# A third table of sums, another order of the last experts, and stores issued from ScalarE

## The chip, the core and the metric

The kernel runs on one core of a Trainium2 chip. The core has TensorE (PE: matrix products and transposes), VectorE (DVE), ScalarE (ACT), GpSimd (POOL) and SyncE (SP), and sixteen DMA engines between its SBUF and HBM. SP, ACT and POOL can issue transfers, each from its own queue and in the order of that queue. An instruction that waits holds up all that stands behind it on its engine. The metric is the time of one execution on the device, in microseconds (us); lower is better.

## The reference, cut to what matters

The input `x` has 4 x 512 tokens of 512 numbers, float32. Four layers are added to it one after the other: an expert with quantised weights, an FFN whose weights come from a table of 16 numbers, a state-space scan, and last a mixture of 32 experts, which is what the change touches:

```python
probs = softmax(x @ gate_w);  w, sel = top_k(probs, 8);  w = w / sum(w)
# each token is sent to its 8 experts; xg holds the tokens of expert e
g = einsum("ech,ehi->eci", xg, w_gate)
u = einsum("ech,ehi->eci", xg, w_up)
y = einsum("eci,eih->ech", silu(g) * u, w_down)
out = zeros.at[t_slot].add(w_slot[:, None] * y)   # summed by token
return x + out
```

An expert's inner width is 192. Each token is in eight experts, so every row of the result is `x` plus eight weighted rows `y`.

## The kernel before, in words

The tokens lie in SBUF as `x[128, 16, 512]`: sixteen tiles of 128 tokens. Batches 0 and 1 are the lower half (tiles 0 to 7), batches 2 and 3 the upper half (tiles 8 to 15). Early in the kernel, between the table lookups of the FFN's weights (`lut_weights`), `scratch` makes the tables in HBM that the experts' results are summed in, and `clear` writes zeros into them (L677 to L686): six stores of three tiles for each table, kept in SP's program order.

An expert's work is a generator, `expert` (L877), in four stages: (1) SP loads its weights and POOL gathers its tokens' rows from `xln` in blocks of 128 (`xg`); (2) TensorE transposes each block, ACT and VectorE in turn copy it to `exT`; (3) TensorE forms gate and up products in PSUM, ACT applies a tanh (L941), and VectorE does two multiplications (L942, L943) to get `h`; (4) TensorE multiplies `h` with the down weights (L954, L958), ACT (even blocks, L967) or VectorE (odd blocks, L965) scales the rows by the gates into `ey`, and POOL scatters them, adding, into a table of sums in HBM (L968). The scatters of one expert come in the order of blocks 0, 2, 1, 3, 4 in the code (a group is multiplied together), for three blocks 0, 1, 2. Two scatters into one table wait for one another, the second being issued when the first has landed; two tables, used by even and odd blocks, take turns.

Experts 0 to 7 are run twice. The first part, with the tokens of the lower half (at most 320 places), runs early beside the routing of the last batch. The second part takes the tokens of the upper half, again 320 places: three blocks. The other 24 experts run once with 576 places, five blocks. The list `calls` (L1125 to L1127) holds the 24 full experts and the eight second parts: 8, 0b, 9, 1b, ..., 15, 7b, and then 16 to 31. `pipeline` (L977) steps through them: for each call the loads of the call two further on and stage 3, then the transposes of the next call and stage 4.

At the end, each token's sum has to be added to `x` and the result stored. The last five and a part of the last but one expert's scatters are put into `sums[1]` (L1129), so that `sums[0]` is complete sooner. `weave` (L1134) then mixes the last expert's two steps with `add_sums(tp, 0, False)`: eight pieces of two tiles, each read from `sums[0]` by SP into a buffer `acc` (six buffers) and added to `x` by VectorE (L1003). `add_sums(tp, 1, True)` follows when the last scatter has landed: eight pieces of `sums[1]`, read by SP (L999), added to `x` into the buffer `acc`, and stored from there by SP (L1005).

The order of the code is not yet that of an engine. A planner takes the instructions, estimates from costs of its own when each will be ready, and writes one fixed list for each engine: among instructions that it thinks ready, the one earlier in the code goes first. On the chip each engine goes through its list in order, waiting where data is not there. A DMA is an entry in the list of the engine that issues it.

```python
sums = [two] * (len(calls) - 2) + [two[:4] + k.sums[1:], k.sums[1:] * 5]
run(islice(late, 2 * len(calls) - 2))
weave((late, 2), (k.add_sums(tp, 0, False), NT // 2))
run(k.add_sums(tp, 1, True))
```

After all this the kernel reads a flag and, only if some expert had more tokens than places, would do the layer anew (`in_full`).

Of the kernel before, what the change touches and what calls it, by code (L numbers as in the profile page):

```python
# [16 lines left out]
F32 = mybir.dt.float32  # L17
# [5 lines left out]
ALU = mybir.AluOpType  # L23
# [4 lines left out]
P = 128  # L28
NB = 4
S = 512  # L30
HID = 512
NT = NB * S // P
# [16 lines left out]
SLOTS = 576  # L49
EARLY = 8  # L50
ROOM = (320, 320)
LO = 32
ROW = HID + NE
LN_EPS = 1e-5
# [5 lines left out]
class Kernel:  # L60
# [556 lines left out]
    def routing_constants(self, rp):  # L617
# [31 lines left out]
        nc.vector.memset(self.room, float(SLOTS))  # L649
        for g, n in enumerate(ROOM):  # L650
            nc.vector.memset(self.room[:, g, :EARLY], float(n))
# [8 lines left out]
    def scratch(self, c):  # L660

        nc = self.nc

        self.xln = [
            self.dram.tile([n * S + 1, ROW], F32, name=f"xln{g}") for g, n in enumerate((NB // 2, NB))
        ]
        zero = c.tile([P, ROW], F32, name="zero")
        nc.vector.memset(zero, 0.0)
        for xln in self.xln:
            nc.sync.dma_start(out=xln[0:1, :], in_=zero[0:1, :ROW])  # L670

        self.sums = [self.dram.tile([NB * S + 2 * P, HID], F32, name=f"sums{i}") for i in range(2)]
        self.kept = self.dram.tile([NB * S, HID], F32, name="kept")
        yield
        yield from self.clear(zero)

    def clear(self, zero):  # L677

        nc = self.nc
        for s in self.sums:  # L680
            for a in range(0, NT + 2, 3):
                z = nc.sync.dma_start(
                    out=s.rearrange("(a p) d -> p a d", p=P)[:, a : a + 3, :],
                    in_=zero[:, :HID].unsqueeze(1).to_broadcast([P, 3, HID]),
                )
                self.tc.keep_in_program_order(z)  # L686
                yield
# [302 lines left out]
            next(e)  # L990
            yield

    def add_sums(self, tp, i, out):

        nc = self.nc
        for a in range(0, NT, 2):
            s = tp.tile([P, 2, HID], F32, tag="acc", name="acc")
            r0 = 1 + a * P
            nc.sync.dma_start(  # L999
                out=s, in_=self.sums[i][r0 : r0 + 2 * P, :].rearrange("(i p) d -> p i d", p=P)  # L1000
            )
            x = self.x[:, a : a + 2, :]
            nc.vector.tensor_tensor(s if out else x, s, x, ALU.add)  # L1003
            if out:
                nc.sync.dma_start(  # L1005
                    out=self.t["out"].rearrange("b (i p) d -> p (b i) d", p=P)[:, a : a + 2, :], in_=s
                )
            yield

    def in_full(self, rp, ep, tp):  # L1010

        nc = self.nc
        zero = ep.tile([P, 2 * HID], F32, tag="exT", name="zero")
        nc.vector.memset(zero, 0.0)
        run(self.clear(zero))
        nc.sync.dma_start(out=self.x, in_=self.kept.rearrange("(i p) d -> p i d", p=P))
        table = ep.tile([P, NE // 4, CAP // LO], F32, tag="xg", name="table", bufs=10)
        nc.vector.memset(table, 0.0)
        for b in range(NB):
            run(self.place(rp, b, self.mask(rp, self.one_hot(rp, b)), self.seen[1], table, None))  # L1020
        toks = self.slots(rp, [table], 0, NE, CAP, "f")
        for e0 in range(0, NE, NE // 2):
            at = self.slot_tokens(rp, toks[:, :, e0 : e0 + NE // 2], CAP, "f")
            run(
                self.pipeline(
                    self.expert(ep, e, (self.xln[1], *at, lo // P), e - e0, HID, self.sums[:1] * 5)
                    for e in range(e0, e0 + NE // 2)
                    for lo in range(0, CAP, HID)
                )
            )  # L1030
        run(self.add_sums(tp, 0, True))


def run(steps):
    for _ in steps:
        pass
# [15 lines left out]
def weave(*streams):  # L1052

    streams = [[0, n, g] for g, n in streams]
    while streams:
        s = min(streams, key=lambda s: s[0] / s[1])
        s[0] += 1
        if next(s[2], StopIteration) is StopIteration:
            streams.remove(s)


@with_exitstack
def tile_kernel(ctx: ExitStack, tc: tile.TileContext, t: dict):
    k = Kernel(tc, t)
    k.constants(ctx)
    scan = ExitStack()
    with ExitStack() as early:
        with ExitStack() as ffn:
            wp = ffn.enter_context(tc.tile_pool(name="wp", bufs=1, side="right"))
            with ExitStack() as first:  # L1070
                k.banks(first, t=2, m=2, y=2, d=2)
                ap = first.enter_context(tc.tile_pool(name="ap", bufs=2))
                sq = staggered([k.smooth_quant(ap, b) for b in range(NB)], 15)
                with ExitStack() as lut:
                    lc = lut.enter_context(tc.tile_pool(name="lc", bufs=1, side="right"))
                    lp = lut.enter_context(tc.tile_pool(name="lp", bufs=2, side="right"))
                    k.lut_tables(lc, wp)
                    lookups = k.lut_weights(lp, k.jobs)
                    weave((islice(sq, 40), 40), (islice(lookups, 48), 48))
                    k.tile_rows(wp, lc)  # L1080
                    weave((islice(sq, 48), 48), (lookups, 4 * len(k.jobs) - 48), (k.scratch(lc), 14))

                pp = ffn.enter_context(tc.tile_pool(name="pp", bufs=1, side="right"))
                k.scan_weights(pp)
                k.prep_tag = "y"
                preps = 2 * KH + 1
                weave((k.prepare(pp, pp, 0), preps), (sq, 30 * NB - 88))
            k.banks(early, t=2, m=2, y=1, d=3)
            k.prep_tag = "t"
            bp = ffn.enter_context(tc.tile_pool(name="bp", bufs=2, side="right"))  # L1090
            rp = ctx.enter_context(tc.tile_pool(name="rp", bufs=1))
            mp = scan.enter_context(tc.tile_pool(name="mp", bufs=2))
            k.routing_constants(rp)
            steps = (TPB // 2) * (NIC + 3)
            units = KH * 16
            routes = 2 * (TPB + 1)

            ffn_ = chain(*(k.lut_ffn(bp, b) for b in range(NB)))
            run(islice(ffn_, 4))
            for b in range(NB):  # L1100
                n = steps
                streams = [(k.scan(mp, b), units), (islice(ffn_, n), n)]
                if b + 1 < NB:
                    streams.append((k.prepare(pp, (pp, mp)[(b + 1) % 2], b + 1), preps))
                if b:
                    run(k.gate(mp, b - 1))
                    streams.append((k.route(rp, b - 1), routes))
                if b == NB - 1:
                    tok = k.slots(rp, k.tables[:1], 0, EARLY, ROOM[0], "a")
                    at = k.slot_tokens(rp, tok, ROOM[0], "a")  # L1110
                weave(*streams)
        ep = ctx.enter_context(tc.tile_pool(name="ep", bufs=2, side="right"))
        k.gu_tag = "m"
        full, nc = SLOTS // P, tc.nc
        two = [k.sums[j % 2] for j in range(full + 1)]
        first = k.pipeline(k.expert(ep, e, (k.xln[0], *at, 0), e, ROOM[0], two) for e in range(EARLY))
        weave((chain(k.gate(mp, NB - 1), k.route(rp, NB - 1)), KH + routes), (first, 2 * EARLY))
    scan.close()
    k.banks(ctx, t=4, g=4)
    k.gu_tag = "g"  # L1120
    tp = ctx.enter_context(tc.tile_pool(name="tp", bufs=6))
    at = k.slot_tokens(rp, k.slots(rp, k.tables, EARLY, NE, SLOTS, "u"), SLOTS, "u")
    at_b = k.slot_tokens(rp, k.slots(rp, k.tables[1:], 0, EARLY, ROOM[1], "b"), ROOM[1], "b")
    k.overflow(rp)
    calls = [(e, at, e - EARLY, SLOTS) for e in range(EARLY, NE)]  # L1125
    for e in range(EARLY):
        calls.insert(2 * e + 1, (e, at_b, e, ROOM[1]))  # L1127

    sums = [two] * (len(calls) - 2) + [two[:4] + k.sums[1:], k.sums[1:] * 5]  # L1129
    late = k.pipeline(  # L1130
        k.expert(ep, e, (k.xln[1], *at, 0), col, n, s) for (e, at, col, n), s in zip(calls, sums)
    )
    run(islice(late, 2 * len(calls) - 2))
    weave((late, 2), (k.add_sums(tp, 0, False), NT // 2))  # L1134
    run(k.add_sums(tp, 1, True))
    more = nc.values_load(k.more[0:1, 0:1], min_val=0, max_val=1)  # L1136
    with tc.If(more):
        k.in_full(rp, ep, tp)
# [51 lines left out]
```

## Time and profile before

| | us |
|---|---|
| median of 3 runs | 1964.97 (1963.19 to 1970.44) |
| profiled execution | 1967.59 |
| its span, first to last instruction | 1965.8 |
| TensorE busy in the span | 1667.2 (85%) |
| VectorE busy | 1192.7 (61%) |
| GpSimd busy | 999.0 (51%) |
| ScalarE busy | 712.7 (36%) |
| last expert's last output written by ACT | 1915.68, for 0.68 |
| last scatter issued | 1929.31 |
| first read of the final eight pieces | 1933.10 |

A time in the profile is counted from the start of the span. A line of a timeline gives start, duration, engine, line of the code, operation, the tile written and the tiles read, how many, and in brackets the idle time before it and what ended that. A line of the chain gives start, duration, and what the end of the kernel waited for in that stretch. In the forty slices of the page each digit is a tenth of busy share; `PEclk` is the clock that TensorE was granted, and a slice is 49 us long. DMA busy time is not that of an instruction: the line of a DMA on an engine's queue is its issue, and the data lands later.

### The profile page before, as it was taken

To read this page: it belongs to the slowest core of one execution; us is meant where nothing else is said; L and a number is where in the kernel's file an instruction comes from. 1 tells how busy PE (TensorE), PEld (TensorE's weight loads), DVE (VectorE), ACT (ScalarE), POOL (GpSimd) and SP (SyncE) were. 2 spreads that over 40 slices of the span, in tenths; PEclk is the share of its full clock that TensorE was granted. 3 is DMA by queue.
4 is the path that set the end of the run, shared out by engine and by line. 5 is a ranking of instruction groups with operands and counts; after the bars stand their busy time and mean duration, and the time that the engine had idled before them with its cause. 6 is when DMAs were issued, how large, how long until landed. Compare 5 with 4: busy or idle time off the path is not lost. (4 is left out here: it accounts for less than half of the span.)

```text
span 1965.8 us, 25002 instructions
## 1 busy us (share of the span) xinstructions
PE 1667.2 (85%) x8845; PEld 984.2 (50%) x8845; DVE 1192.7 (61%) x2029; ACT 712.7 (36%) x1345; POOL 999.0 (51%) x824
## 2 busy tenths in 40 slices
PE   4778775899889888888799688799999999999980
PEld 2444332556454545454555344455556566556540
DVE  6887864788799979999889634422222233222231
ACT  1554455535443554355433322222222222222210
POOL 3110113768755875478566543556555555555420
PEclk9889986899999998899999799999999999999985
DMA  9524510889887888788789686688888877877656
GB/s 264 140 80 153 182 50 34 221 201 227 211 234 165 208 212 213 165 200 205 207 198 221 189 210 134 165 180 197 176 181 178 185 164 160 180 169 170 111 128 186
DMA packets 187673, 346.69 MB, mean 176 GB/s; under 512 B 41698, under 2 KB 88130, under 8 KB 187540
## 3 DMA queue, kind: packets, MB, share of 16 engines
q1 hardware_dynamic: 147332, 251.96, 48.6%
q0 software_dynamic: 39952, 92.66, 23.7%
q8 instruction: 72, 1.18, 0.3%
q10 hardware_dynamic: 256, 0.39, 0.1%
q14 instruction: 61, 0.50, 0.1%
HBM read 277.08 MB, written 76.32 MB: 180 GB/s over the span
## 5 line engine op out<-in xcount | busy, mean ns | idle before, releaser
L968 POOL DMA_INDIRECT sums<-ey,to x168 | 260.8, 1552 | 311.5 <-DMA sums<-ey,to 123.4
L925 PE MATMUL pg<-exT,egu 128*128 128x320 f32 (+1 forms) x1536 | 402.5, 419 | 15.5 <-DVE eh L943 7.6
L563 POOL TENSOR_TENSOR dBu<-d,BC 128x512 f32<-128x512 f32 x256 | 330.8, 1302 | 112.1 <-DMA d<-dts 79.8
L925 PEld LDWEIGHTS pg<-exT,egu 128*128 128x128 f32 x1536 | 289.2, 191 | 131.8 <-issue 38.0
L568 DVE TENSOR_TENSOR_SCAN st<-st,dBu 128x512 f32<-128x512 f32 x192 | 230.7, 1218 | 29.9 <-POOL dBu L563 25.3
L561 ACT ACTIVATE st<-d,A 128x512 f32<-128x512 f32 x256 | 173.5, 689 | 189.9 <-DVE sc L569 122.1
L375 PE MATMUL pgu<-xT,wg 128*128 128x256 f32 (+1 forms) x704 | 189.4, 412 | 30.6 <-DVE h L385 26.1
L900 POOL DMA_INDIRECT xg<-xln,tokens x168 | 162.0, 964 | 90.8 <-issue 37.9
L942 DVE SCALAR_TENSOR_TENSOR eh<-eh,pg 128x320 f32<-128x320 f32 (+5 forms) x144 | 61.1, 425 | 230.6 <-ACT eh L941 229.3
L954 PE MATMUL po_e<-ed,eh 128*128 128x512 f32 (+1 forms) x336 | 172.9, 633 | 13.2 <-ACT ey L967 6.2
L340 PE MATMUL pw<-oh,lut_t 128*32 128x344 bf16 (+1 forms) x2052 | 127.0, 359 | 65.5 <-DVE oh L334 65.2
L375 PEld LDWEIGHTS pgu<-xT,wg 128*128 128x128 f32 (+1 forms) x704 | 132.3, 198 | 97.3 <-DVE h L385 39.0
L375 PE MATMUL pgu<-xT,wu 128*128 128x256 f32 (+1 forms) x704 | 179.4, 397 | 0.0
L967 ACT ACTIVATE ey<-po_e,gates 128x512 f32<-128x512 f32 (+1 forms) x104 | 68.8, 684 | 303.8 <-PE po_e L958 151.1
L965 DVE TENSOR_SCALAR ey<-po_e,gates 128x512 f32<-128x512 f32 x64 | 45.9, 748 | 209.0 <-PE po_e L958 209.0
L391 PE MATMUL po_f<-wd,h 128*128 128x512 f32 (+1 forms) x352 | 159.8, 610 | 2.6 <-DVE h L385 2.2
L375 PEld LDWEIGHTS pgu<-xT,wu 128*128 128x128 f32 (+1 forms) x704 | 138.5, 199 | 25.8 <-issue 2.9
L569 DVE TENSOR_TENSOR sc<-st,BC 128x512 f32<-128x512 f32 x192 | 127.7, 681 | 19.8 <-PE py L579 18.9
L573 POOL TENSOR_TENSOR sc<-sc,BC 128x512 f32<-128x512 f32 x64 | 83.2, 1300 | 110.0 <-DVE sc L566 83.1
L958 PE MATMUL po_e<-ed,eh 64*128 64x512 f32 (+1 forms) x336 | 114.8, 638 | 0.0
L340 PEld LDWEIGHTS <-lut_t 128*32 128x32 bf16 x2052 | 56.3, 102 | 113.2 <-issue 74.0
L391 PEld LDWEIGHTS po_f<-wd,h 128*128 128x128 f32 (+1 forms) x352 | 68.0, 196 | 86.3 <-issue 80.6
(260 smaller groups left out, 2195.0 us busy)
## 6 DMA issues: line engine op xcount, KB each, us to landing
d<-dts SPq DMA_DIRECT2D x256, 512.0 KB, 6.3
egu<-in_w_gate SPq DMA_DIRECT2D x40, 384.0 KB, 3.8
ix<-idx_b SPq DMA_DIRECT2D x16, 688.0 KB, 5.4
egu<-in_w_up SPq DMA_DIRECT2D x40, 256.0 KB, 5.2
ed<-in_w_down SPq DMA_DIRECT2D x40, 256.0 KB, 4.0
ed<-in_w_down SPq DMA_DIRECT2D x80, 128.0 KB, 4.5
sums<-zero SPq DMA_DIRECT2D x12, 768.0 KB, 6.7
dts<-dt POOLq DMA_DIRECT2D x16, 512.0 KB, 4.5
```

The costliest lines, as they stand in the source:

```text
L340: nc.tensor.matmul(pt[i][32 * c : 32 * c + 32, :step], lhsT=self.lut_t[:, j, g, :], rhs=oh[:, c * n + i * step : c * n + (i + 1) * step], ...
L375: nc.tensor.matmul(pg[:m, j * W : (j + 1) * W], lhsT=w[:, k, c * P : c * P + m], rhs=xT[:, k, :], start=k == 0, stop=k == KH - 1,)
L391: nc.tensor.matmul(po, lhsT=h[:m, c, i * P : (i + 1) * P], rhs=self.wd[:m, c, :], start=c == 0, stop=c == NIC - 1,)
L561: nc.scalar.activation(st, d[:, 0, :], AF.Exp, scale=self.A[:, i : i + 1])
L563: product = nc.gpsimd.tensor_tensor(dBu, d[:, 1, :], BC[:, 0, :], ALU.mult)
L568: nc.vector.tensor_tensor_scan(st, st, dBu, 0.0, ALU.mult, ALU.add)
L569: nc.vector.tensor_tensor(sc, st, BC[:, 1, :], ALU.mult)
L900: nc.gpsimd.indirect_dma_start(out=xg[:m, :], out_offset=None, in_=xln, in_offset=bass.IndirectOffsetOnAxis(ap=tokens[:m, lo + j, col : co ...
L925: nc.tensor.matmul(pg[i][:, :hs], lhsT=w[:, k, i * P : (i + 1) * P], rhs=xT[:, k, z : z + hs], start=k == 0, stop=k == KH - 1,)
L954: nc.tensor.matmul(po[j][:m, :], lhsT=h[:, 0, b : b + m], rhs=wd[:, 0, :], start=True, stop=False)
L958: nc.tensor.matmul(po[j][:m, :], lhsT=h[r : r + R, 1, b : b + m], rhs=wd[r : r + R, 1, :], start=False, stop=True)
L968: nc.gpsimd.indirect_dma_start(out=sums[j], out_offset=bass.IndirectOffsetOnAxis(ap=to[:m, lo + j, col : col + 1], axis=0), in_=y[:m, :], ...
```

## The change

A third table `sums[2]` is made, and only its last twelve tiles of rows are cleared (`a0 = NT // 2 - 2` tiles are skipped), which takes four stores; `clear` so has sixteen steps instead of twelve, and the weave that spreads them counts 18 in place of 14. The second parts of experts 6 and 7 (`LAST = 2`) leave their places in the list and come at its very end, after expert 31: the list is 8, 0b, ..., 13, 5b, 14, 15, 16, ..., 31, 6b, 7b. All scatters of these two, three blocks each, go into `sums[2]`; all others, expert 31's too, take turns between `sums[0]` and `sums[1]`. Since second parts hold only tokens of the upper half, the rows of the lower half are then complete in the first two tables.

`add_sums` takes a list of tables and a range of tiles. It now always adds into `x`, table after table, and where it stores, it stores from `x` and issues the store on ACT's queue instead of SP's. The last two calls' four steps are woven with eight pieces: four of the lower half, which add both tables and store, and four of the upper half, which add both tables only. What follows when the last scatter has landed is four pieces of the upper half: read from `sums[2]`, added and stored. `in_full` calls the new form.

```diff
+LAST = 2
-        self.sums = [... for i in range(2)]
+        self.sums = [... for i in range(3)]
...
-        for s in self.sums:
-            for a in range(0, NT + 2, 3):
+        for s, a0 in zip(self.sums, (0, 0, NT // 2 - 2)):
+            for a in range(a0, NT + 2, 3):
...
-    def add_sums(self, tp, i, out):
+    def add_sums(self, tp, sums, a0, a1, out):
-        for a in range(0, NT, 2):
-            s = tp.tile([P, 2, HID], F32, tag="acc", name="acc")
-            r0 = 1 + a * P
-            nc.sync.dma_start(out=s, in_=self.sums[i][r0 : r0 + 2 * P, :]...)
+        for a in range(a0, a1, 2):
             x = self.x[:, a : a + 2, :]
-            nc.vector.tensor_tensor(s if out else x, s, x, ALU.add)
+            for table in sums:
+                s = tp.tile([P, 2, HID], F32, tag="acc", name="acc")
+                r0 = 1 + a * P
+                nc.sync.dma_start(out=s, in_=table[r0 : r0 + 2 * P, :]...)
+                nc.vector.tensor_tensor(x, s, x, ALU.add)
             if out:
-                nc.sync.dma_start(out=self.t["out"]...[:, a : a + 2, :], in_=s)
+                nc.scalar.dma_start(out=self.t["out"]...[:, a : a + 2, :], in_=x)
...
-                    weave(..., (k.scratch(lc), 14))
+                    weave(..., (k.scratch(lc), 18))
...
-    for e in range(EARLY):
+    for e in range(EARLY - LAST):
         calls.insert(2 * e + 1, (e, at_b, e, ROOM[1]))
+    calls += [(e, at_b, e, ROOM[1]) for e in range(EARLY - LAST, EARLY)]
-    sums = [two] * (len(calls) - 2) + [two[:4] + k.sums[1:], k.sums[1:] * 5]
+    sums = [two] * (len(calls) - LAST) + [k.sums[2:] * 3] * LAST
...
-    run(islice(late, 2 * len(calls) - 2))
-    weave((late, 2), (k.add_sums(tp, 0, False), NT // 2))
-    run(k.add_sums(tp, 1, True))
+    run(islice(late, 2 * (len(calls) - LAST)))
+    weave(
+        (late, 2 * LAST),
+        (
+            chain(k.add_sums(tp, k.sums[:2], 0, NT // 2, True), k.add_sums(tp, k.sums[:2], NT // 2, NT, False)),
+            NT // 2,
+        ),
+    )
+    run(k.add_sums(tp, k.sums[2:], NT // 2, NT, True))
```

More of the change, by code (lines that the diff above doesn't have):

```diff
@@ L670, in scratch @@
             nc.sync.dma_start(out=xln[0:1, :], in_=zero[0:1, :ROW])
-        self.sums = [self.dram.tile([NB * S + 2 * P, HID], F32, name=f"sums{i}") for i in range(2)]
+        self.sums = [self.dram.tile([NB * S + 2 * P, HID], F32, name=f"sums{i}") for i in range(3)]
         self.kept = self.dram.tile([NB * S, HID], F32, name="kept")
@@ L991, in pipeline @@
             yield
-    def add_sums(self, tp, i, out):
+    def add_sums(self, tp, sums, a0, a1, out):
         nc = self.nc
-        for a in range(0, NT, 2):
-            s = tp.tile([P, 2, HID], F32, tag="acc", name="acc")
-            r0 = 1 + a * P
-            nc.sync.dma_start(
-                out=s, in_=self.sums[i][r0 : r0 + 2 * P, :].rearrange("(i p) d -> p i d", p=P)
-            )
-            x = self.x[:, a : a + 2, :]
-            nc.vector.tensor_tensor(s if out else x, s, x, ALU.add)
+        for a in range(a0, a1, 2):
+            x = self.x[:, a : a + 2, :]
+            for table in sums:
+                s = tp.tile([P, 2, HID], F32, tag="acc", name="acc")
+                r0 = 1 + a * P
+                nc.sync.dma_start(out=s, in_=table[r0 : r0 + 2 * P, :].rearrange("(i p) d -> p i d", p=P))
+                nc.vector.tensor_tensor(x, s, x, ALU.add)
             if out:
-                nc.sync.dma_start(
-                    out=self.t["out"].rearrange("b (i p) d -> p (b i) d", p=P)[:, a : a + 2, :], in_=s
+                nc.scalar.dma_start(
+                    out=self.t["out"].rearrange("b (i p) d -> p (b i) d", p=P)[:, a : a + 2, :], in_=x
                 )
@@ L1030, in in_full @@
             )
-        run(self.add_sums(tp, 0, True))
+        run(self.add_sums(tp, self.sums[:1], 0, NT, True))
 def run(steps):
@@ L1080, in tile_kernel @@
                     k.tile_rows(wp, lc)
-                    weave((islice(sq, 48), 48), (lookups, 4 * len(k.jobs) - 48), (k.scratch(lc), 14))
+                    weave((islice(sq, 48), 48), (lookups, 4 * len(k.jobs) - 48), (k.scratch(lc), 18))
                 pp = ffn.enter_context(tc.tile_pool(name="pp", bufs=1, side="right"))
```

## The prediction

> **What bounds the kernel now.** I read four views, from the coarse to the fine. First the page's forty slices: TensorE is busy from start to end and then stops in the last slice but one.
>
> ```profile
> PE   4778775899889888888799688799999999999980
> PEclk9889986899999998899999799999999999999985
> DMA  9524510889887888788789686688888877877656
> ```
>
> One slice is 49 us, so the change, which touches the last 90 us, is judged there and not by shares of the span. Second, the chain of work that ended last, in order of time: it holds no arithmetic but one kind of addition.
>
> ```profile
> 1923.70 1.55 DMA sums<-ey,to
> 1929.31 3.73 DMA sums<-ey,to
> ...
> 1934.06 5.57 DMA acc<-sums
> ...
> 1942.79 6.91 DMA acc<-sums
> ...
> 1951.47 5.23 DMA acc<-sums
> ...
> 1958.11 1.23 DVE acc L1003
> ```
>
> The end is set by scatters waiting for one another (to 1933.0), then by eight pieces of a table read, added and stored (to 1959.75), then 6.05 us to the end of the span. Third, POOL's timeline, which shows the scatters of two full experts: number 29 undisturbed, and from 1890.97 those that all go to `sums[1]`.
>
> ```profile
> 1855.48 1.55 POOL L968 DMA_INDIRECT sums<-ey,to  x1 [3.30 <-ACT ey L967]
> 1860.85 1.55 POOL L968 DMA_INDIRECT sums<-ey,to  x1 [3.82 <-issue]
> 1862.71 1.55 POOL L968 DMA_INDIRECT sums<-ey,to  x1 [0.30 <-DVE eh L943]
> 1866.36 1.45 POOL L968 DMA_INDIRECT sums<-ey,to  x1 [2.09 <-DMA sums<-ey,to]
> 1868.65 1.58 POOL L968 DMA_INDIRECT sums<-ey,to  x1 [0.85 <-DVE eh L943]
> ...
> 1890.97 1.55 POOL L968 DMA_INDIRECT sums<-ey,to  x1 [4.41 <-DMA sums<-ey,to]
> 1899.92 1.42 POOL L968 DMA_INDIRECT sums<-ey,to  x1 [7.40 <-DMA sums<-ey,to]
> ```
>
> Two scatters into one table start 5.4 to 5.6 us apart on quiet DMA (1855.48 to 1860.85; 1923.70 to 1929.31), but 8.95 and 6.65 us apart while eight table reads pass (1890.97, 1899.92, 1906.57). I call this a link. Fourth, the timeline of all engines where those reads begin.
>
> ```profile
> 1888.02 9.79 SPq L999 DMA_DIRECT2D acc<-sums  x8
> 1894.61 1.23 DVE L1003 TENSOR_TENSOR x<-acc,x 128x1024 f32<-128x1024 f32 x1 [9.98 <-DMA acc<-sums]
> 1896.34 4.64 PE L925 MATMUL pg<-exT,egu 128*128 128x320 f32 x8 [5.27 <-DVE eh L942]
> ```
>
> The planner put the first addition ahead of products of the last expert. On the chip its data came 6.6 us after the read was issued, VectorE stood still for 9.98 us, TensorE for 5.27, and its granted clock fell from 1.00 (1870 to 1881) to 0.80 (1881 to 1916). This costs little now, since the scatters end later anyway; the same pattern matters more after the change.
>
> **The change, part by part.** *Third table and its clearing:* four more stores of 768 KB, each 0.59 us of SP and landing in a median 6.7 us. They stand between index loads that SP issues 6 to 12 us apart, with DMA at 0.55 from 142 to 246 us. Bounds: nothing, to 4 x 2.3 = 9 us if the DMA engines were the limit there (768 KB at the 330 GB/s of the tail). I take nothing, hidden by the lookups' TensorE and VectorE work.
>
> *Order:* the second parts of experts 6 and 7 leave their places after experts 14 and 15. TensorE's work is the same. Pairs leave it idle 0.2 us in 210, full experts in a row 3.7 in 170 (about 0.5 each, behind the h products); two more in a row cost +1.0 us. When does the last full expert end? Its gate and up products start at 1881.3 now, after eight second parts. One such part is 6.7 (gate, up) + 1.4 (transposes) + 5.0 (down) = 13.1 us, so the start becomes 1881.3 - 26.2 - 0.9 (three transposed blocks stand before it instead of five, for the next call's transposes follow) + 1.0 = 1855.2. Add 11.9 gate and up, 1.4 transposes, 8.1 down: T = 1877.
>
> *When both old tables are complete:* expert 29 ended on TensorE at 1859.4 and its fourth scatter landed about 1871.8 (1866.36 + 5.4), its fifth 1873.9. So `sums[0]` is complete at T + 12.4 = 1889.4 and `sums[1]` at 1891.5. The first read starts about where it does now (1888.0), but TensorE is then deep in the last two second parts rather than in the last full expert.
>
> *Reads and additions beside them:* sixteen reads of 512 KB and four stores, 10.5 MB, where before there were eight reads. At 330 GB/s (what the DMA row shows in slices of this stretch; 512 KB takes 1.6 us) a lower piece takes 4.8 us, an upper piece 3.3. First addition at 1889.4 + 6.6 = 1896, the last at 1896 + 4 x 4.8 + 4 x 3.3 = 1928. A DVE addition itself takes 1.23.
>
> *What is queued behind these waits.* On VectorE the additions stand in the planner's order among the last two experts' products, transposed copies and odd outputs. On ACT four new stores are issued (an ACT issue took 0.31 us, by the row of `xdbl`), each waiting for both additions of its piece; behind them stand the tanh and even outputs that feed the scatters. Before, stores waited on SP alone. Unheld, the first output of expert 6 would be ready at T + 11.8, 1889. Held by the first store, which wants the second or third addition, it comes at 1901 and its scatter at 1902. That is the uncertain value: 1889 to 1902; I take 1902, since the planner showed its optimism about these very reads. Similarly expert 7's products: at one addition per 1.3 us (the alternation with h products in the trace suggests that the planner counts so) some eleven additions precede the last of them, done on the chip at 1896 + 8 x 2.4 + 3 x 1.6 = 1920. The down products then run at half clock (10 us instead of 5), the first output at 1926.5.
>
> *The last chain:* six scatters into `sums[2]`, with the loaded link as the mean of 8.95 and 6.65 = 7.8: 1902, 1909.8, 1917.6; then, when expert 7's output is there, 1926.5, 1933.2, 1938.7; landed 3.75 later, S = 1942.4. Now it is 1933.0.
>
> *The last pieces:* four instead of eight, 4.2 MB instead of 8.4. SP, waiting now in its queue for additions before it may issue more reads, has only reads to issue.
>
> ```profile
> SPq L1005 <- DVE acc L1003: 18.1, 8, 5.0
> ```
>
> The Trainium skill speaks against this step: "DMA: Bandwidth & Descriptors", section "Issuing engines are not separate DMA queues", says that all engines' DMAs run on the same sixteen DMA engines and that a second issuer saves only the time to issue. By that rule I keep the row's pace: 3.8 to the first addition, 4 x (1959.75 - 1936.85) / 8 = 11.5, then 6.05, sum 21.3. By the 18.1 us of waiting I could let all four reads land by +8 (three additions now start 3.8, 5.0 and 6.5 us after the reads): last addition done +9.3, stored +9.6, end +15.7. But the rule's shared engines must still move 4.2 MB, 12.7 us, plus 1.9 to start and the 4.1 between the last traffic and the span's end: 18.7. I take 18; now it is 32.8.
>
> *Sum:* 1942.4 + 18 = 1960.4 against the execution's span of 1965.8: -5.4. Around that span lie 1.8 us (1967.59 in all), which stay. The median of the runs is 2.6 below that execution; I take the difference to the median: 1964.97 - 5.4 = 1959.6, rounded to 1959.
>
> **The rivals.** *Unheld:* the planner leaves expert 6's outputs and expert 7's products ahead of additions and stores. For it: reads wait for scatters that by the planner's own count come after expert 6's products. Against it: the 9.98 us stall. Then the chain starts at 1889 and is bound by links alone: 1889, 1898, 1904.6, 1912.4, 1920.2, 1928, landed 1931.8, end 1949.8: 1949.
>
> *Slower:* the additions stand on VectorE ahead of expert 7's copy of its transposed tokens. All sixteen are done at 1928; then 0.7 for the copy, 13.5 gate and up at half clock, 1.5 products, 7.5 to the first output: scatter at 1951, two more links of 5.5 and 3.75, S = 1966, end 1984, time 1983. It decides against the change from the point where expert 7's first scatter starts later than 1965.8 - 18 - 3.75 - 11 = 1933. If only the products of h are behind all additions, the scatter is at 1937 and the time 1969. For it: VectorE takes instructions in order, and additions were put among products before. Against it: so were products among additions.
>
> *Nothing moves:* the shorter final part (32.8 to 18) is given back by a chain that lands 14.8 us later, at 1948, if every loaded link is 9 us and the first scatter starts after 1905. This lies at the upper end of my own case.
>
> **How the numbers follow.** Faster or slower means 0.5% (9.8 us), about what a measurement of this kernel can tell: below 1955.1 or above 1974.8. My case has 0.50: of it 0.18 faster, 0.31 within, 0.01 slower; its own range is 1951 to 1969, from the loaded link (6.6 to 9 us) and the last part (15.7 to 21.3). Unheld 0.26: 0.25 faster, 0.01 within. Slower mechanism, whole or in part, 0.24: 0.03 within, 0.21 slower. Sums: 0.43, 0.35, 0.22. The range leaves out a little below the unheld case and the worst of the slower one: 1947 to 1976.
>
> **What would show it.** Right: twelve clearing stores become sixteen with no later end of that stage; the last TensorE work well after 1900 at a reduced clock; ACT's longest waits on its own stores; six scatters 6 to 9 us apart, the last landing near 1942; 18 us from there to the end. Wrong: the first of these six at 1889 (unheld), or the fourth later than 1933 (slower); an end of the lookups that moves by several us; or a planner that orders the middle of the kernel anew, which no row here shows.

## The result, and the profile after

The changed kernel takes 1955.16 us, the median of 13 runs (1946.71 to 1964.62), against 1965.36 us (1962.65 to 1976.34) for the kernel before in as many runs. The ratio is 0.9942, with a 95% interval of 0.9924 to 0.9959: 0.6% faster, 10 to 11 us. The profiled execution spans 1953.5 us where the one before spanned 1965.8.

The slices of the page differ at the end: TensorE's last work is now spread out further, and the DMA engines stay busy (0.7 and 0.6 in the last two slices against 0.5 and 0.6 before).

```profile
PE   4778875899889888898888588899999999999981
PEclk9989986899999898899899799999999999999995
DMA  9535611889887887778789696688887877778776
...
sums<-zero SPq DMA_DIRECT2D x16, 768.0 KB, 6.6
```

The sixteen clearing stores cost nothing that can be seen: the last lookup product is at 272.4 us here and was at 275.4 before; over all profiles of this document it lies between 275.4 and 279.7 with twelve stores and between 272.4 and 280.9 with sixteen. The tail is another thing. The chain of what ended last, in order of time (start, duration, what was waited for), from the last full expert on:

```profile
1876.50 5.16 DMA sums<-ey,to
...
1882.39 5.40 DMA sums<-ey,to
...
1887.81 3.62 DMA acc<-sums
...
1891.52 1.24 DVE x L1004
...
1892.78 0.46 ACTq L1006
...
1893.36 0.70 ACT ey L969
...
1894.32 8.65 DMA sums<-ey,to
...
1903.70 7.92 DMA sums<-ey,to
...
1912.36 7.34 DMA sums<-ey,to
...
1920.43 4.71 DMA sums<-ey,to
...
1925.87 4.84 DMA sums<-ey,to
...
1931.44 3.58 DMA sums<-ey,to
...
1936.65 9.21 DMA acc<-sums
```

Read it from the top: the last scatter into `sums[1]` by expert 31 lands at 1887.8; the first piece's read from that table waited for it; its addition lets ACT issue the first store (L1006); only behind that store does ACT write expert 6's first output (L969), and then six scatters follow one another. The last lands at 1935.0, and 18.5 us later the span ends. Before, the last landing was at 1933.0 with 32.8 us to go. So the last part became 14.3 us shorter and the chain landed 2.0 us later; part of the 12.3 us between the two spans arose earlier, as the next section shows.

How the last two experts were held is seen in the timeline of all engines (start, duration, engine and line; in brackets the idle time before and what ended it):

```profile
1889.01 1.22 DVE L1004 TENSOR_TENSOR x<-acc,x 128x1024 f32<-128x1024 f32 x1 [8.80 <-DMA acc<-sums]
1890.15 0.68 DVE L917 COPY exT<-pt_g 128x512 f32<-128x512 f32 x1
1890.89 9.19 PE L927 MATMUL pg<-exT,egu 128*128 128x320 f32 x24 [4.97 <-DVE exT L917]
1892.78 0.46 ACTq L1006 DMA_DIRECT2D out<-x  x1
1893.36 0.69 ACT L969 ACTIVATE ey<-po_e,gates 128x512 f32<-128x512 f32 x1 [12.00 <-DVE x L1004]
```

VectorE stood 8.80 us in front of the first addition, with expert 7's transposed copy behind it; TensorE lost 4.97 us there and did the 24 products in 9.19 us where the same 24 took 6.73 for expert 6. ACT stood for 12.00 us until the second addition released the store. Not all of that is the hold: by the prediction's estimate an output that nothing holds would have come 11.8 us after the last full expert's end, at 1884.8 here, so about 8.5 us are.

### The profile page after: what moved, and what is told of

Read it like the earlier page. It is cut to its first block, busy times and chain, and to the rows that moved or that the text cites. A ratio compares the mean times of both kernels' runs of the same rounds, so it can differ in the third digit from the quotient of the medians.

```text
span 1953.5 us, 25018 instructions
## 1 busy us (share of the span) xinstructions
PE 1661.3 (85%) x8836; PEld 983.6 (50%) x8845; DVE 1196.9 (61%) x2033; ACT 711.6 (36%) x1345; POOL 1001.9 (51%) x824
## 4 chain that ended last, share of the span: by engine, by line
PE 35%; DMA 7%; DVE 5%; issue 2%; ACT 1%; POOL 1%; SPq 0%; ACTq 0%; POOLq 0%; DVEq 0%
PE pg L927 17%; PE po_e L956 8%; PE po_e L960 5%; PE pt_g L915 3%; DMA sums<-ey,to 2%; DMA xg<-xln,tokens 2%; DMA d<-dts 2%; DVE st L569 1%; DVE sc L570 1%; DMA acc<-sums 1%; POOL xg L902 0%; POOL dBu L564 0%; DVE lo_i L803 0%; PE pl L712 0%; DVE eh L945 0%
## 5 line engine op out<-in xcount | busy, mean ns | idle before, releaser
L944 DVE SCALAR_TENSOR_TENSOR eh<-eh,pg 64x128 f32<-64x128 f32 (+5 forms) x144 | 61.1, 425 | 223.5 <-ACT eh L943 222.4
L969 ACT ACTIVATE ey<-po_e,gates 128x512 f32<-128x512 f32 (+1 forms) x104 | 68.7, 684 | 290.2 <-PE po_e L960 143.4
L392 PEld LDWEIGHTS po_f<-wd,h 128*128 128x128 f32 (+1 forms) x352 | 68.3, 197 | 87.3 <-issue 80.3
```

The source lines that it names most:

```text
L392: nc.tensor.matmul(po, lhsT=h[:m, c, i * P : (i + 1) * P], rhs=self.wd[:m, c, :], start=c == 0, stop=c == NIC - 1,)
```

## The experiments

Executions of one kernel differ by more than ten us (the runs above), and the profiles show that much of it arises before the tail, so I also give, for each profile, the time from a **mark** to the end of the span. The mark is the start of the gate and up products of expert 6's second part: 1873.0 in the changed kernel, 1889.3 in another that is the same up to there. For kernels with another order the mark is worked out from the prediction's stage lengths (before: 1881.3 - 26.2 - 0.9 + 11.9 + 1.4 + 8.1 = 1875.6; with one or three second parts at the end, 13.15 us before or after the first one's start). A blank stands where the chain that ended last does not hold the last scatter. Each ratio is to the kernel before as it ran beside that version.

| kernel | ratio to before, interval | mark to end | of it after the last landing |
|---|---|---|---|
| before | 1 | 90.2 | 32.8 |
| order alone | 0.9995, 0.9969 to 1.0022 | 85.7 | 33.0 |
| stores from ACT alone | 0.9985, 0.9965 to 1.0006 | 85.2 | 28.3 |
| changed | 0.9942, 0.9924 to 0.9959 | 80.5 | 18.5 |
| changed, again | 0.9953, 0.9927 to 0.9980 | 79.5 | 15.8 |
| changed, stores from SP | 0.9961, 0.9940 to 0.9981 | 81.5 | 20.8 |
| changed, three read buffers | 0.9940, 0.9916 to 0.9963 | 80.8 | 17.1 |
| additions behind the experts | 0.9913, 0.9880 to 0.9946 | 72.0 | 15.5 |
| the same, ten buffers | 0.9912, 0.9879 to 0.9945 | 72.9 | |
| the same, two tables at the end | 0.9916, 0.9898 to 0.9935 | 73.0 | |
| two tables and ten buffers | 0.9929, 0.9896 to 0.9963 | 71.1 | |
| one second part last | 0.9934, 0.9913 to 0.9956 | 74.1 | |
| the same, additions behind | 0.9925, 0.9898 to 0.9952 | 71.8 | |
| three second parts last | 0.9955, 0.9936 to 0.9974 | 80.3 | 16.0 |

Two readings come from the table alone. By the mark, the last landing came after 57.4 us before and 62.1 us in the changed kernel: 4.6 us later, against a last part that is 14.3 shorter. That leaves 9.7 us for the change; the other 2.6 of the 12.3 between the spans lie ahead of the mark. And the last part follows the number of its pieces: eight pieces take 32.8 and 33.0 us with stores on SP and 28.3 with stores on ACT, four take 20.8 on SP and 18.5 or 15.8 on ACT. The last two are the same kernel, so a single profile fixes this part to no better than 3 us; from the mark to the end the same two agree within about 1 us.

**The order alone.** The kernel before with expert 6's and 7's second parts last, everything else as it was.

```diff
-    for e in range(EARLY):
+    for e in range(EARLY - 2):
         calls.insert(2 * e + 1, (e, at_b, e, ROOM[1]))
+    calls += [(e, at_b, e, ROOM[1]) for e in range(EARLY - 2, EARLY)]
-    sums = [two] * (len(calls) - 2) + [two[:4] + k.sums[1:], k.sums[1:] * 5]
+    sums = [two] * (len(calls) - 2) + [k.sums[1:] * 3] * 2
-    run(islice(late, 2 * len(calls) - 2))
-    weave((late, 2), (k.add_sums(tp, 0, False), NT // 2))
+    run(islice(late, 2 * len(calls) - 4))
+    weave((late, 4), (k.add_sums(tp, 0, False), NT // 2))
```

> The kernel before with only the new order of calls (second parts of experts 6 and 7 last, all their scatters into sums[1]); stores, number of tables and the eight final pieces as before. Theory (the gain is the shorter last part, less a chain of scatters that lands slightly later): the eight final pieces stay at about 32.8 us, so the only gain is an earlier landing of the chain. Without stores on ACT the first of the six scatters is not held (about 1887 instead of 1894) and only eight reads load the links, so the chain lands near 1925 to 1930 and the end comes 3 to 8 us before 1965.8: ratio to before 0.996 to 0.9985. Rival A (the order itself is what pays): the whole gain, ratio 0.994. Rival B (order alone costs, since six links follow where five did): ratio 1.000 to 1.003.

Ratio 0.9995 with 5 us of interval to either side. Its profile spans 1973.8 us because the mark lies at 1888.1. From there the chain lands at 52.8 us and the eight pieces take 33.0, as expected:

```profile
1937.09 3.73 DMA sums<-ey,to
...
1941.84 5.46 DMA acc<-sums
...
1950.59 7.29 DMA acc<-sums
...
1960.20 5.64 DMA acc<-sums
...
1965.93 1.23 DVE acc L1003
```

That the order by itself brings the whole gain (0.994) is refuted; whether it brings the 4.5 us of the profile or nothing, these runs can't tell.

**Stores from ACT alone.** The kernel before with one word changed.

```diff
-                nc.sync.dma_start(
+                nc.scalar.dma_start(
                     out=self.t["out"]
```

> The kernel before with one edit: the eight final stores are issued from ACT's queue instead of SP's. By the rule that issuing engines share the same sixteen DMA engines the gain is at most the issue time of eight stores, 8 x 0.37 = 3 us (ratio 0.9985 to 1.000). Theory: 8.4 MB at 330 GB/s, 25.4, with 1.9 to start and 4.1 at the end, is 31.4 against 32.8: 1 to 3 us (ratio 0.998 to 1.000). Rival (SP's 18.1 us of waiting in front of reads was on the path): 6 us or more, ratio 0.997 or less.

Ratio 0.9985, a gain of 3 us that the interval doesn't hold apart from nothing or from 7. The last landing is at 1934.7, and 28.3 us remain instead of 32.8: 4.5 us less, between the 3 of the one theory and the 6 of the other. Where SP had waited 18.1 us for additions, its queue now waits for what frees the buffers it reads into (waits of SP's queue after 1930):

```profile
SPq L999 <- DMA out<-acc: 9.5, 2, 8.8
```

The stores are still in front of the last reads, now by the buffers that they empty. In the changed kernel that can't be: there are four reads and six buffers.

**The changed kernel with its stores back on SP.**

```diff
-                nc.scalar.dma_start(
+                nc.sync.dma_start(
                     out=self.t["out"]
```

> The changed kernel with its stores back on SP's queue (all other edits kept). Theory: ACT's outputs and tanh for the last two experts are no longer queued behind stores, so expert 6's first scatter starts near 1885 instead of 1894.3; the second one is still held on VectorE behind additions until about 1897; the last landing comes 2 to 5 us earlier, the final part stays: 1 to 5 us below the changed kernel, ratio to before 0.991 to 0.994. Rival (the separate queue is what lets the reads run ahead): reads stand behind waiting stores on SP, the additions and expert 7 come later, 2 to 6 us above the changed kernel, ratio 0.995 to 0.997.

Ratio 0.9961, from the mark 81.5. Expert 6's first scatter does start sooner, 13 us after the mark instead of 21.4, but it gains nothing, since the next one waits for VectorE:

```profile
1889.51 1.56 POOL L970 DMA_INDIRECT sums<-ey,to  x1 [1.88 <-ACT ey L969]
1901.08 2.28 POOL L970 DMA_INDIRECT sums<-ey,to  x1 [10.02 <-DVE ey L967]
1910.85 1.42 POOL L970 DMA_INDIRECT sums<-ey,to  x1 [7.49 <-DMA sums<-ey,to]
```

The chain lands 1.3 us sooner by the mark and the last part is 2.3 us longer. The theory's gain is not there; the rival's size (2 to 6 us worse) fits the medians, though the intervals overlap. ACT's queue for stores is worth at most a few us, and in the early part it is a hold like VectorE's.

**Additions and early stores behind the last expert.** VectorE's sixteen early additions are pinned behind expert 7's last output there, and ACT's stores behind its last output on ACT (`last_dve` and `last_act` are these two outputs; what is written under `issue_after` goes behind them in the engine's list); reads are free to run ahead into six buffers.

```diff
-    weave((late, 2 * LAST), (chain(... lower half ..., ... upper half ...), NT // 2))
+    run(late)
+    with tc.issue_after(k.last_dve.ins), tc.issue_after(k.last_act.ins):
+        run(k.add_sums(tp, k.sums[:2], 0, NT // 2, True))
+        run(k.add_sums(tp, k.sums[:2], NT // 2, NT, False))
```

> The changed kernel with the sixteen additions placed on VectorE behind the last output of expert 7, and the four early stores on ACT behind ACT's last output; reads are issued as before (six buffers). Theory (additions and stores hold up the last two experts, and this delays the chain of scatters by some 9 us): the first scatter starts near 1885, expert 7's first near 1905 to 1908 with TensorE at full clock, the last lands near 1926 to 1930 instead of 1935; the end is 4 to 9 us below the changed kernel: ratio to before 0.990 to 0.992. Rival (the chain is set by the loaded links alone, the DMA load only moves to another place): within 2 us of the changed kernel, ratio 0.993 to 0.995. Second rival: the additions, begun only near 1898, end after the chain and the last part begins later: above the changed kernel.

Ratio 0.9913, and 72.0 us from the mark where the changed kernel needs 80.5. With ten buffers (below) it repeats: 0.9912 and 72.9. TensorE does both sets of 24 products at full speed, and the first scatter starts 13.0 us after the mark (timelines of TensorE and POOL):

```profile
1889.26 6.73 PE L927 MATMUL pg<-exT,egu 128*128 128x320 f32 x24
1902.16 6.73 PE L927 MATMUL pg<-exT,egu 128*128 128x320 f32 x24
```
```profile
1902.27 1.56 POOL L974 DMA_INDIRECT sums<-ey,to  x1 [1.51 <-ACT ey L971]
1907.78 1.55 POOL L974 DMA_INDIRECT sums<-ey,to  x1 [3.95 <-DVE eh L944]
1917.20 1.84 POOL L974 DMA_INDIRECT sums<-ey,to  x1 [7.87 <-DMA sums<-ey,to]
1926.85 1.97 POOL L974 DMA_INDIRECT sums<-ey,to  x1 [7.81 <-DMA sums<-ey,to]
1935.91 1.78 POOL L974 DMA_INDIRECT sums<-ey,to  x1 [7.08 <-DMA sums<-ey,to]
1942.17 1.43 POOL L974 DMA_INDIRECT sums<-ey,to  x1 [4.49 <-DMA sums<-ey,to]
```

So the hold was real and cost about 8 us from the mark: 5.6 by an earlier landing, 3.0 by a shorter last part (15.5 against 18.5; but the changed kernel itself had 15.8 once). The ratios differ by less, some 6 us, and their intervals overlap; beside each other on one chip, the changed kernel took 1960.26 us (12 runs) and the version with ten buffers 1953.61 (6 runs). How the 8 us divide between VectorE and ACT is not settled: with the stores on SP, above, ACT's hold was gone, and VectorE's alone kept the end where it was, but SP's queue then held reads behind stores; additions pinned behind with ACT's stores still in front were not tried. The start is 8.4 us sooner and the landing 5.6, because more of the links are now long: they are 5.5, 9.4, 9.7, 9.1 and 6.3 us.

**Three buffers for the reads.** `bufs=6` becomes `bufs=3` in the changed kernel.

> The changed kernel with three buffers for table reads instead of six, so at most three reads of 512 KB are in flight. If the loaded link (8 to 9.4 us against 5.5) comes from the depth of reads queued on the DMA engines: links of 6.5 to 7.5 while additions run, the chain lands 2 to 5 us sooner. If it comes from the engines' bandwidth being used up at all: links stay at 8 to 9. In both cases reads run less ahead, so the end may not follow: ratio to before 0.992 to 0.998.

Ratio 0.9940, 80.8 us from the mark: no change. With at most three reads in flight the five links are 10.6, 8.3, 5.9, 7.0 and 5.3 us:

```profile
1898.24 2.53 POOL L970 DMA_INDIRECT sums<-ey,to  x1 [11.39 <-ACT ey L969]
1908.83 2.19 POOL L970 DMA_INDIRECT sums<-ey,to  x1 [8.07 <-DMA sums<-ey,to]
1917.17 1.42 POOL L970 DMA_INDIRECT sums<-ey,to  x1 [6.16 <-DMA sums<-ey,to]
1923.07 1.57 POOL L970 DMA_INDIRECT sums<-ey,to  x1 [4.47 <-DMA sums<-ey,to]
```

Together they take 37.2 us, where the changed kernel's five take 37.1: the third is 2.2 us shorter, the first and fourth are longer. So fewer reads in flight did not bring the chain in sooner. What makes one link long and another short stays open: other reads and writes beside it are not enough, for this run's third link took 5.9 us with the DMA engines busy 0.92 of the time, and the first one of the version with the additions behind took 5.5 us with them busy all of it.

**One and three second parts at the end.** `LAST = 1` and `LAST = 3` in the changed kernel.

> The changed kernel with one second part at the end instead of two (LAST = 1): three links in the last chain instead of six, but the first two tables are complete one second part (13.1 us) later, so the sixteen reads and four stores (32 us) end later. Theory: the reads, not the chain, then set when the last part can start: last landing near the end of the additions, end within 2 us of the changed kernel, ratio 0.993 to 0.996. Rival (the chain alone counts: three links of 8.7 less, 13.1 later): 8 us or more below the changed kernel, ratio 0.990 or less.

> The changed kernel with three second parts at the end (LAST = 3): nine links in the last chain. The tables are complete 13.1 us sooner, so the loaded time ends sooner; first scatter 13.1 us sooner, four links of 8.7 and four of 5.5, landing 69 us after the mark at which it is 62 in the changed kernel: 6 us above the changed kernel, ratio to before 0.996 to 0.999. Rival (cover is what counts, more of it is better): at or below the changed kernel, ratio 0.994 or less.

One: 0.9934, 74.1 us. Here the bound is another. Over the 46 us from the first read on, the DMA engines are busy 0.97 of the time (the answer for a stretch; the last columns are TensorE's clock, the DMA share and GB/s). The changed kernel's stretch from its first read stands below it, with 0.79:

```profile
1892.60:1939.00 46.40, 1.82 (x6) 0.19 (x2) 25.08 (x21) 1.25 (x2) 5.34 (x4) 0.56 0.97 331
```
```profile
1883.80:1949.50 65.70, 18.16 (x43) 8.22 (x42) 28.14 (x29) 3.66 (x7) 10.12 (x7) 0.64 0.79 248
```

The reads set that end, as the theory said, though from the mark it is 6 us shorter, more than it expected. Three: 0.9955 and 80.3 us, with the landing at 64 us after the mark instead of the expected 69, since the additions were over at 38 us and the later links ran at 4.4 to 5.5. Both ratios lie within the interval of the changed kernel, which has two.

**Two tables for the last chain, more buffers, one second part unheld.** The first gives expert 6 and expert 7 a table each at the end (a fourth table is made, and cleared like the third), with additions and stores behind the experts; then that with ten buffers; ten buffers with one table; and `LAST = 1` with additions behind the expert.

```diff
-    sums = [two] * (len(calls) - LAST) + [k.sums[2:] * 3] * LAST
+    sums = [two] * (len(calls) - LAST) + [k.sums[2:3] * 3, k.sums[3:] * 3]
...
-        run(k.add_sums(tp, k.sums[:2], NT // 2, NT, False))
+        run(k.add_sums(tp, k.sums[:3], NT // 2, NT, False))
-    run(k.add_sums(tp, k.sums[2:], NT // 2, NT, True))
+    run(k.add_sums(tp, k.sums[3:], NT // 2, NT, True))
```

> The kernel with additions and early stores behind the last expert's outputs, and besides a table of sums of its own for each of the last two experts (expert 6 into the third, expert 7 into a fourth, also cleared); the third is read with the early pieces of the upper half, the fourth at the end. If the chain of six links into one table sets the end (theory): the two chains of three run side by side, the last landing comes 5 to 9 us sooner and the end follows: ratio to before 0.986 to 0.989. Rival (the sixteen DMA engines set the end: 20 instead of 16 early reads, 6.4 us more at 330 GB/s, and the last reads wait behind them): within 2 us of the kernel with one table, ratio 0.990 to 0.993.

> The same with a table of its own for each of the last two experts and ten buffers. With six buffers it took 73.0 us from the mark. Theory (with two tables the bytes set the end: 24 reads and 8 stores, 16.8 MB at 330 GB/s is 51 us, and 6 to start and end): reads begin 11 us after the mark and with ten buffers do not pause, so 67 to 70 us, ratio 0.987 to 0.989. Rival (something else, such as the two chains under load): 72 us or more, ratio 0.990 to 0.993.

> The kernel with additions and early stores behind the last expert's outputs, with ten buffers for table reads instead of six. From the mark (start of expert 6's second gate and up products) that kernel took 72.0 us with six. Theory (with one table the chain of six loaded links is what ends last, at 56 us after the mark): more reads ahead do not help, 70 to 73 us, ratio to before 0.990 to 0.992. Rival (SP's queue, blocked from the sixth read until the first addition, is what ends last): 66 to 69 us, ratio 0.988 to 0.989.

> One second part at the end (LAST = 1), with additions and early stores behind its outputs. With LAST = 1 alone the DMA engines were busy from the first table read to the end: 20 reads and 8 stores, 14.7 MB, 44.5 us at 330 GB/s and 6 to start and end. Theory (bytes): holding or not holding the expert changes nothing, within 2 us of LAST = 1 alone (74 us from the comparable mark), ratio 0.991 to 0.995. Rival (the held expert delays the end there too): 4 us or more below, ratio 0.990 or less.

> The changed kernel once more, on the chip of the three kernels beside it, so that they can be set against it directly. Expected: ratio to before 0.992 to 0.996, and in the profile some 80.5 us (79 to 82) from the start of expert 6's second gate and up products to the end of the span, wherever that start lies.

Two tables: 0.9916 and 73.0 us, so nothing over one table. The last scatter starts 49.8 us after the mark instead of 52.9, but four reads more fill the engines:

```profile
1883.00:1941.00 58.00, 13.78 (x43) 6.27 (x42) 32.58 (x32) 3.77 (x7) 10.93 (x6) 0.66 0.97 316
```

Ten buffers with it gave 71.1, between what the two theories had; the ratio of 0.9929 shows no gain. Ten buffers with one table gave 72.9, as expected of a chain of scatters. With one second part and nothing held, 71.8 against 74.1, and a ratio of 0.9925 against 0.9934: neither theory's number, and no difference that these runs resolve. The changed kernel came out at 0.9953 and 79.5 us once more.

All versions without a held expert, or with one second part, lie between 71 and 74 us from the mark. The version with the additions behind the last experts beats both given kernels by the medians, and the changed one by 7 to 8 us from the mark, with six buffers and with ten.

## Why the prediction was right, and where its steps were off

*Bound and mechanism.* The end was set as said: scatters into one table one after the other, then pieces read, added and stored. That the last part would pay for a somewhat later landing is what happened: 32.8 to 18.5 (predicted 18), landing from 1933.0 to 1935.0 (predicted 1942.4). The forecast of -5.4 us was about half of what came, 10.2 us between the medians and 12.3 between the spans; 1959 was forecast, 1955.16 measured, inside the case's own range of 1951 to 1969. The last part's agreement within 0.5 us is in part luck: the same kernel had 15.8 in another execution. The landing was 7.4 us sooner than predicted: 4.0 from T (its end of the last full expert), 3.6 from the hold, and the chain after its first scatter nearly as long as predicted (1.6 longer up to the fourth scatter, 1.3 shorter behind it).

*The order's cost of +1.0 and T = 1877.* Off by 4 us. Of these, 1.4 are the cost of +1.0 (0.5 us of idle time for each full expert) and rounding; the other 2.6 lie between the two executions, of which this one was 3.0 ahead at the end of the lookups. The cost itself is not seen here: in the profile after, TensorE is busy 350.0 of the 350 us from 1500 to 1850; before it was 342.5:

```profile
1500.00:1850.00 350.00, 342.53 (x1373) 209.50 (x1372) 99.95 (x189) 86.62 (x237) 194.36 (x155) 1.00 0.77 168
```
```profile
1500.00:1850.00 350.00, 350.00 (x1408) 215.87 (x1408) 102.72 (x192) 88.21 (x238) 197.36 (x156) 1.00 0.79 169
```

This is no merit of the change. From 1280 to 1500 it was the other way round (219.8 of 220 before, 215.9 after), and among kernels with the same order up to there, one with its additions behind the experts had 342.9 and the order alone had 349.95. What decides it from one execution to the next was not tried and stays open.

*When the tables are complete, and the additions.* Predicted T + 12.4 and T + 14.5; with the measured T of 1873.0, the first read was issued at T + 10.8 and the second table complete at T + 14.8. The last early addition ended at T + 48.8, predicted T + 51 (two reads of 1.6 make 3.2 for an upper piece, not the 3.3 used there: 0.4 us in the sum).

*The hold.* The step that I took at its upper end was right in kind: the first store on ACT held expert 6's first output, and VectorE's first addition held expert 7's copy. In size it was T + 20.4 for the output, not T + 24, because the first addition began at T + 16.0 instead of T + 19: the first table was complete 1.6 us sooner, and its read took 5.2 us to the addition instead of 6.6. The second addition followed after 2.5 us, close to the 2.4 of the step. Holding everything behind the experts shows its price, about 8 us.

*The links.* 7.8 us was the term; the loaded ones measured 9.4, 8.7 and 8.1, the last two 5.4 and 5.6. Expert 7's first scatter came 2.7 us after the time at which three links of 7.8 would have let it go (1917.7, measured 1920.4), while its output had been written by 1915.9. So the chain was never short of outputs, where I had let expert 7's output delay it to 1926.5 (T + 49.5; measured T + 42.9). Nine additions, not eleven, stood before its last product of h, and its down products took 6.8 us, not the 10 of half clock throughout.

*The rule on issuing engines.* The rule that the prediction cites from the Trainium skill ("DMA: Bandwidth & Descriptors", "Issuing engines are not separate DMA queues") has a second issuer save issue time alone: 8 x 0.37 = 3 us for the kernel before. The profile of that edit alone shows 4.5 us off the last part, and the runs show 3 with an interval from -1 to 7; whether the gain is the rule's 3 us or somewhat more, they can't tell. The rule was still the better guide to the size: SP's 18.1 us of waiting were not 18.1 us of path.

*The rivals.* Unheld was the case that didn't come, but its estimate stood: chain from 13 us after the mark, end about 10 us below the changed case, and the experiment that forces it gave 8 from the mark and some 6 by the ratios. The slower rival had the right place (the copy stood behind an addition) and the wrong amount: one addition, not sixteen.

## What to carry to other kernels

Where work is put beside other work "to hide it", ask what each of its waiting instructions holds up on its own engine: here nine of the sixteen additions and four stores, placed by a planner that thought their data ready, stood in front of outputs of the very experts whose scatters set the end, and putting them behind cost no arithmetic and gave some 8 us from the mark (some 6 by the ratios, whose intervals overlap). Then ask what is left: once nothing was held, fewer links or more buffers or another table all ended within about 3 us of one another. With one second part or two tables the DMA engines were then busy 0.97 of the time; with one table the chain of scatters was what ended last. And where executions differ by 10 us, a mark in the profile just ahead of the change separates versions that the medians alone hardly do.

## What the runs showed of the hardware that was not expected

A scatter that adds into a table in HBM, waited for before the next, takes 5.4 to 5.6 us from start to start on quiet DMA engines (5.44 and 5.57 in the changed kernel, with the engines busy 0.38 and 0.37 of the time) and mostly 8 to 10.6 beside table reads, but 5.5 and 5.9 there as well. Limiting the reads in flight from six to three (512 KB each) left the sum of the last chain's five links as it was, 37.2 us against 37.1. The profiles of kernels whose list of calls up to the mark is the same reached it anywhere from 1872.1 to 1889.3 us; why was not found.
